# Layer 2 keys in written order with statistics a batch ahead; layer 0 preparation with a third TensorE tap and sums of offset excess

## The chip, the core and the metric

The kernel runs on one core of one Trainium2 chip. The metric is device time in microseconds (us) of one execution, taken as the median over the runs. All data is float32.

The core's engines are TensorE (PE for the matmuls, PEld for its weight loads), VectorE (DVE), ScalarE (ACT), GpSimd (POOL) and SyncE (SP), which issues nearly all of the transfers. Each engine works through its own queue in order and waits on semaphores.

## What is computed

The input is eight images of 56 x 56 pixels with 128 channels. Four layers follow one another. Two parts of them matter here.

Layer 0 is a deformable convolution with a small MLP behind it. Its first part, which the kernel calls the preparation, computes for each image a projection and, from a depthwise 3 x 3 convolution, the offsets and masks of the sampling:

```python
xp = x @ w_in + b_in                                   # what is sampled
h  = conv_3x3_depthwise(x, dw_w) + dw_b                # nine taps per channel
h  = gelu(batch_norm(h))
offset = (h @ w_off + b_off)                           # 4 groups x 9 points x 2
mask   = softmax((h @ w_msk + b_msk), axis=-1)         # over the 9 points
y = sample_bilinear(xp, grid + offset, mask)           # deformable sampling
```

Layer 1 is a whitening of the channels. Layer 2 starts with self-attention in which keys, queries and values are one and the same projection:

```python
n = (t - mean(t)) / sqrt(var(t) + 1e-5)                # per token, 3136 tokens an image
h = n @ W_k.T                                          # 8 heads of 16
scores = h @ h.T / sqrt(16)                            # per head
t = t + softmax(scores) @ h @ W_o.T
```

Feed-forward parts with experts and a linear attention (layer 3) follow; the change doesn't touch them.

## The kernel before

The kernel works through its stages one after another: preparation of layer 0, sampling and MLP of layer 0, whitening, keys of layer 2, attention of layer 2, experts, and layer 3 with its experts. Some stages have an order written out by hand (`tc.manual_schedule`, the attention is one); in the others a planner orders each engine's instructions by the program's order and by estimated times. Both stages that the change touches are left to the planner.

**Preparation of layer 0** (in `conv_layer`, lines 200 to 398). A loop goes over the images, with three of them in flight. `image` (L256) loads an image, transposes it on TensorE into 28 columns of tokens (L266), copies it on ScalarE into a padded plane `xp` (L271) and stores a reordered copy `xT` (L276, L279). Two images share one padded plane; there are two such planes. `first_taps` does the first `NTE` of the nine taps of the depthwise convolution as matmuls with diagonal matrices (L315, seven chunks of 128x448), and ScalarE copies the sums to `acc` (L322). `other_taps` does the other taps on VectorE, one instruction over 128x3136 each (L327). `projection` (L288, L295) runs once per pair of images, in two halves: TensorE multiplies, VectorE adds the bias, and the result goes to `strips` in DRAM. `hidden` is the GELU on ScalarE (L341). `offsets` multiplies on TensorE (L356), adds the bias on VectorE (L363) into `om`, takes the largest and the smallest offset of the image into `far` (L365, L366), does the softmax of the masks (`mask_softmax`, L430 to L435, with its Exp on ScalarE at L432), and stores `om`.

The rows and columns around `strips` are filled with zeros by transfers that ScalarE issues (L240, L245).

At the end the largest of all `far` decides whether every offset is within one pixel (L398). If it is, `sample_near` runs, otherwise a general and much slower form.

**Keys of layer 2** (`attention_keys`, L1039 to L1133). A loop goes over the eight images, here called batches. For each:

1. The tokens are loaded from `y` into `t` in two transfers of 56 partitions each, in pieces of 512 bytes, so that token 112 i + p stands at partition p, column i (L1062); and they are written to `tok` in the order of the tokens (L1063).
2. VectorE takes statistics of 28 columns (L1067, L1068) and adds the epsilon (L1140); POOL takes the power of -1/2 (L1141, in `rsqrt`).
3. VectorE normalizes column by column (L112), TensorE transposes (L121), ScalarE copies groups of four columns to `xT` (L122).
4. TensorE computes the keys in 14 chunks of 128x448 (L1083). VectorE and ScalarE take turns in scaling and copying them to `kT` (L1091, L1087). `kT` has one buffer and is stored in two transfers (L1094).
5. TensorE computes the values in 25 tiles (L1098). VectorE and ScalarE take turns in copying them to `va` (L1108, L1106), which is stored in two transfers (L1110).
6. POOL squares the values (L1117), VectorE sums them and takes the largest (L1119, L1120). These become a bound that decides which form of the attention runs.

All transfers are issued by SP. `query_bound` (L2080 to L2104), a short chain for layer 3 that begins with a load on SP (L2088), stands behind the keys in the program; the attention follows it.

Of the kernel before, what the change touches and what calls it, by code (L numbers as in the profile page):

```python
# [8 lines left out]
F32 = mybir.dt.float32  # L9
# [9 lines left out]
S = IH * IW  # L19
# [16 lines left out]
R4 = 4 * C  # L36

NPX = 6
NTE = 2


WB, WCOLS, WSTEP, WITER, WEPS = 64, NB * S * C // 64, 9, 5, 0.01
# [85 lines left out]
def conv_layer(tc, k, x, w, z):  # L128
# [3 lines left out]
    with ExitStack() as ctx:  # L132
# [63 lines left out]
        gam = row_bc(nc, cp, w["gamma2"], T, "gam2r")  # L196
        nc.vector.tensor_tensor(q.sft2, q.sft2, gam, ALU.mult)

        far = cp.tile([T, 2 * n_batch], F32, name="far")
        near = cp.tile([1, 1], I32, name="near")  # L200
        with ExitStack() as pre:
            ip = pre.enter_context(tc.tile_pool(name="l0i", bufs=1))
# [11 lines left out]
                "b_om",  # L214
            )
            b_om = b_om.unsqueeze(1).to_broadcast([T, GT, 3 * GP])

            dw = ip.tile([C, 9], F32, name="dw")
            nc.sync.dma_start(dw, w["dw_w"].rearrange("c a b d -> c (a b d)"))
# [13 lines left out]
            nc.vector.tensor_tensor(bn_t, bn_t, bn_s, ALU.mult)  # L233
            nc.vector.tensor_tensor(bn_t, bn_t, bn_b, ALU.add)

            zero = ip.tile([NX * n_batch, 2 * SW * C], F32, name="zero")
            nc.gpsimd.memset(zero, 0.0)
            rows = q.strips.rearrange("n k y s c -> (n k) y (s c)")
            for y in (0, VW - 2):
                nc.scalar.dma_start(  # L240
                    rows[:, y : y + 2].rearrange("k y s -> k (y s)"), zero
                )
            for n in range(n_batch):
                for at in (q.strips[n, 0, :, :2], q.strips[n, NX - 1, :, SW - 2 :]):
                    nc.scalar.dma_start(  # L245
# [104 lines left out]
            def offsets(n, hT):  # L350

                om = hp.tile([T, NT, 3 * GP], F32, name="om")
                for r in range(PH):
                    p = ps.tile([T, GT, 3 * GP], F32, tag="m", name="p_om")
                    for i in range(GT):
                        nc.tensor.matmul(  # L356
                            p[:, i, :],
                            hT[:, r, i].rearrange("p a b -> p (a b)"),
                            w_om,
                            start=True,  # L360
                            stop=True,
                        )
                    nc.vector.tensor_tensor(om[:, r * GT : (r + 1) * GT, :], p, b_om, ALU.add)  # L363
                off = om[:, :, : 2 * GP]
                nc.vector.tensor_reduce(far[:, 2 * n : 2 * n + 1], off, AX.XY, ALU.max)  # L365
                nc.vector.tensor_reduce(  # L366
                    far[:, 2 * n + 1 : 2 * n + 2], off, AX.XY, ALU.min, negate=True
                )
                mask_softmax(nc, hp, om)
                nc.sync.dma_start(q.om[n], om)  # L370


# [22 lines left out]
            nc.tensor.transpose(p, top, k.ident[:T, :T])  # L395
            one = ip.tile([1, 1], F32, name="far_one")
            nc.vector.tensor_reduce(one, p, AX.X, ALU.max)
            nc.vector.tensor_scalar(near, one, 1.0, None, ALU.is_le)  # L398

        taken = nc.values_load(near[0:1, 0:1], min_val=0, max_val=1)  # L400
        with tc.If(taken > 0) as both:
# [634 lines left out]
    return [(t, min(128, S - 128 * t)) for t in range(KT)]  # L1036


def attention_keys(tc, k, w, yv, tok, kT_out, va_out, low, small):  # L1039

    nc = tc.nc
    n_b = yv.shape[1]
    with ExitStack() as ctx:
        cp = ctx.enter_context(tc.tile_pool(name="akc", bufs=1))
        bp = ctx.enter_context(tc.tile_pool(name="akb", bufs=2))
        ps = ctx.enter_context(tc.tile_pool(name="akp", bufs=6, space=PSUM))
        vas = []  # L1050
        for i in range(2):
            va = cp.tile([128, 2, KT, 4, 32], F32, name=f"va{i}")
# [3 lines left out]
            vas.append(va)  # L1056
        tops = cp.tile([128, n_b], F32, name="tops")
        wk = w.wk.rearrange("p h d -> p (h d)")
        for n in range(n_b):
            t_sb = bp.tile([T, NT, C], F32, name="t")  # L1060
            for h in range(2):
                nc.sync.dma_start(t_sb[h * IW : (h + 1) * IW], yv[h, n])  # L1062
            nc.sync.dma_start(tok[n].rearrange("(t p) c -> p t c", p=T), t_sb)  # L1063
            mv = bp.tile([T, NT, 2], F32, name="mv")
            st = bp.tile([T, NT, 6], F32, name="st")
            for i in range(NT):
                nc.vector.bn_stats(st[:, i], t_sb[:, i])  # L1067
                nc.vector.bn_aggr(mv[:, i], st[:, i])  # L1068
            rs = rsqrt(nc, k, bp, mv, NT)
            xT = bp.tile([C, S], F32, name="xT")  # L1070
            for g in range(NG):
                xn = bp.tile([T, GT, C], F32, name="xn")
                for i in range(GT):
                    normalize(nc, xn[:, i], t_sb[:, g * GT + i], mv, rs, g * GT + i)
                transpose_group(
                    nc, k, ps, "m", xT[:, g * QC : (g + 1) * QC], xn, nc.scalar.copy
                )
            kT = bp.tile([128, 2, S], F32, name="kT", bufs=1)
            for g in range(2):
                for c in range(NG):  # L1080
                    cols = slice(c * QC, (c + 1) * QC)
                    p = ps.tile([128, QC], F32, tag="m", name="p_h")
                    nc.tensor.matmul(  # L1083
                        p, wk[:, g * 128 : (g + 1) * 128], xT[:, cols], start=True, stop=True
                    )
                    if c % 2:
                        nc.scalar.activation(  # L1087
                            kT[:, g, cols], p, AF.Identity, bias=w.one16, scale=DK**-0.25
                        )
                    else:  # L1090
                        nc.vector.tensor_scalar(  # L1091
                            kT[:, g, cols], p, DK**-0.25, w.one16, ALU.mult, ALU.add
                        )
                nc.sync.dma_start(kT_out[n, g], kT[:, g])  # L1094
            va = vas[n % 2]
            for t, m in key_tiles():
                p = ps.tile([128, 2, 4, DK], F32, tag="m", name="p_v")
                nc.tensor.matmul(  # L1098
                    p[:m].rearrange("p g j d -> p (g j d)"),
                    xT[:, t * 128 : t * 128 + m],  # L1100
                    w.wv,
                    start=True,
                    stop=True,
                )
                if t % 2:
                    nc.scalar.copy(va[:m, :, t, :, :DK], p[:m])  # L1106
                else:
                    nc.vector.tensor_copy(va[:m, :, t, :, :DK], p[:m])  # L1108
            for g in range(2):
                nc.sync.dma_start(va_out[n, g], va[:, g].rearrange("p t j d -> p (t j d)"))  # L1110

            sq = bp.tile([128, 2 * KT * 4, DK], F32, name="sq", bufs=1)
            v = va.rearrange("p g t j d -> p (g t j) d")[:, :, :DK]
            nc.gpsimd.tensor_tensor(sq, v, v, ALU.mult)  # L1117
            top = bp.tile([128, 2 * KT * 4], F32, name="top")
            nc.vector.tensor_reduce(top, sq, AX.X, ALU.add)  # L1119
            nc.vector.tensor_reduce(tops[:, n : n + 1], top, AX.X, ALU.max)  # L1120

        col = cp.tile([128, 1], F32, name="top_c")
        nc.vector.tensor_reduce(col, tops, AX.X, ALU.max)
# [12 lines left out]
def rsqrt(nc, k, pool, mv, n):  # L1136

    m = mv.shape[0]
    rs = pool.tile([m, n], F32, name="rs")
    nc.vector.tensor_scalar(rs, mv[:, :, 1], EPS, None, ALU.add)  # L1140
    nc.gpsimd.tensor_tensor(rs, rs, k.mhalf[:m, :n], ALU.pow)  # L1141
    return rs
# [1081 lines left out]
def token_layers(tc, k, a, y, out):  # L2224
# [3 lines left out]
    with ExitStack() as ctx:  # L2228
# [13 lines left out]
        with tc.tile_pool(name="tlr", bufs=1) as rp:  # L2242
# [33 lines left out]
            yv = y.rearrange("(t a) n w c -> a n w t c", a=2)  # L2276
            low = cp.tile([128, 1], F32, name="low")
            small = cp.tile([1, 1], I32, name="small")
            attention_keys(tc, k, w, yv, tok, kT_d, va_d, low, small)
# [108 lines left out]
```

## Time and profile before

| | us |
|---|---|
| median of 3 runs | 7665.0 (7655.8 to 7673.1) |
| the profiled execution | 7657.9 |
| its span, first to last instruction | 7656.2 |
| layer 0 preparation, 0 to 433 of the span | 433 |
| layer 0 sampling and MLP, 433 to 1437 | 1004 |
| layer 1 whitening, 1437 to 1580 | 143 |
| layer 2 keys with their weights, 1580 to 1949 | 369 |
| layer 2 attention, 1949 to 6545 | 4596 |
| the rest | 1111 |

Over the span the mean granted clock of TensorE is 0.908 of full speed. TensorE is busy 84% of it, VectorE 69%, ScalarE 54%, POOL 38%; but these are means over stages with different limits, and a stage's own windows have to be read for what limits it.

A line of a group reads: line of the kernel, engine, operation, output and inputs with their shapes, number of instructions; then busy time in us and the mean duration of one in ns; then the idle time of the engine just before them, and whom it waited for. A matmul of float32 leaves two records in the trace. A line of the waits reads: who waited, for whom: us in total, how many times, the longest.

### The profile page before, as it was taken

The numbers are of one execution on the slowest core, as the hardware profiler recorded it, in microseconds if no ns is written. First come the engines' busy times: TensorE is split into PE (matmuls) and PEld (weight loads), VectorE is DVE, ScalarE is ACT, GpSimd is POOL, SyncE is SP. The second block draws the span as 40 slices with busy tenths as digits, with TensorE's granted clock in tenths as the row PEclk, the third lists the DMA queues.
The fourth block names the chain that finished last, engine by engine and source line by source line (L and its number), as shares of the span: only waits on it lengthen the run. The fifth ranks groups of instructions, "written<-read, shape, count | busy, mean of one in ns | idle before, by whom it ended". The sixth has DMA issues, their size and how long they took to land. (4 is left out here: it accounts for less than half of the span.)

```text
span 7656.2 us, 158331 instructions
## 1 busy us (share of the span) xinstructions
PE 6459.4 (84%) x59947; PEld 2867.8 (37%) x59947; DVE 5281.9 (69%) x9840; ACT 4163.3 (54%) x6499; POOL 2939.2 (38%) x2555
## 2 busy tenths in 40 slices
PE   6659999565899999999999999999999999556764
PEld 4446666333233333333333323323323323235542
DVE  7975564356677777777777777777777777356761
ACT  4424444122566666666666666666666666146750
POOL 0001111022344444444444444444444444333763
PEclk9768899776999999999999999999999999789877
DMA  5453343376787877778777778878778777544544
GB/s 156 135 121 78 85 97 65 83 227 215 191 207 191 197 188 192 197 190 195 197 191 192 197 187 197 198 188 196 195 191 197 190 185 181 198 111 113 137 134 142
DMA packets 737846, 1287.45 MB, mean 168 GB/s; under 512 B 119235, under 2 KB 504645, under 8 KB 730053
## 3 DMA queue, kind: packets, MB, share of 16 engines
q1 hardware_dynamic: 727092, 1260.77, 65.5%
q0 software_dynamic: 6144, 12.60, 0.5%
q8 instruction: 486, 7.96, 0.4%
q10 hardware_dynamic: 3824, 3.68, 0.2%
q14 instruction: 300, 2.45, 0.1%
HBM read 286.04 MB, written 197.81 MB: 63 GB/s over the span
## 5 line engine op out<-in xcount | busy, mean ns | idle before, releaser
L1260 ACT ACTIVATE e<-p_s 128x768 f32<-128x768 f32 (+2 forms) x3712 | 2887.8, 830 | 1588.2 <-PE p_s L1252 1320.1
L1298 POOL COPY x<-sq 32x1152 f32<-32x1152 f32 x1792 | 2062.2, 1151 | 2017.6 <-PE p_s L1252 1241.2
L1271 DVE STREAM_TRANSPOSE sq<-e 128x768 f32<-128x768 f32 x2688 | 2434.3, 950 | 516.0 <-ACT e L1260 258.9
L1252 PE MATMUL p_s<-q,kT 32*128 32x384 f32 (+2 forms) x14848 | 1892.8, 548 | 37.8 <-ACT e L1260 21.9
L1305 PE MATMUL av<-e,va 128*32 128x384 f32 (+2 forms) x14848 | 1646.5, 515 | 13.3 <-DVE acc L1328 8.3
L1305 PE MATMUL avx<-x,va 128*32 128x384 f32 x10752 | 1134.3, 494 | 62.2 <-issue 38.9
L1252 PEld LDWEIGHTS p_s<-q,kT 32*128 32x128 f32 (+1 forms) x14848 | 649.3, 181 | 1266.1 <-issue 837.7
L1305 PEld LDWEIGHTS av<-e,va 128*32 128x32 f32 (+1 forms) x14848 | 294.0, 108 | 1030.7 <-issue 936.9
L1305 PEld LDWEIGHTS avx<-x,va 128*32 128x32 f32 x10752 | 351.5, 111 | 642.4 <-issue 601.9
L609 POOL TENSOR_TENSOR rs<-rs,mhalf 112x4 f32<-112x4 f32 x112 | 116.1, 1036 | 789.8 <-DVE rs L608 789.8
L1324 DVE TENSOR_TENSOR acc<-acc,avx 128x384 f32<-128x384 f32 x336 | 183.8, 547 | 232.5 <-PE avx L1305 229.5
L121 PE MATMUL p_tr<-ident,xn 112*128 112x112 f32 x672 | 133.5, 338 | 188.6 <-DVE xn L112 141.8
L1141 POOL TENSOR_TENSOR rs<-rs,mhalf 112x4 f32<-112x4 f32 (+2 forms) x136 | 167.9, 1235 | 249.6 <-DVE ntop L1986 123.5
L525 ACT COPY wT<-p_w 88x448 f32<-88x448 f32 x152 | 137.8, 921 | 193.1 <-PE p_w L523 193.1
L2034 ACT ACTIVATE xn<-t,ms,rs 112x128 f32<-112x128 f32 x448 | 185.2, 487 | 76.2 <-DVE ms L2027 76.2
L327 DVE SCALAR_TENSOR_TENSOR acc<-xp,dw,acc 128x3136 f32<-128x3136 f32 x56 | 193.9, 3471 | 29.8 <-ACT acc L322 29.7
L637 PE MATMUL p_f<-x1T,w 128*128 128x448 f32 x448 | 209.4, 593 | 4.4 <-DVE x1T L632 2.8
L121 PEld LDWEIGHTS p_tr<-ident,xn 112*128 112x128 f32 x672 | 97.5, 167 | 282.0 <-issue 186.6
L523 PE MATMUL p_w<-ident,wide 112*88 112x112 f32 x896 | 146.6, 303 | 58.6 <-DMA px<-strips 34.1
L1394 POOL TENSOR_TENSOR rs_b<-rs_b,mhalf 128x3 f32<-128x3 f32 (+1 forms) x72 | 58.5, 815 | 356.5 <-DVE rs_b L1393 347.0
L621 DVE TENSOR_TENSOR y<-y,p_rs 128x448 f32<-128x448 f32 x112 | 69.3, 619 | 182.2 <-PE p_rs L614 182.2
L122 ACT COPY xT<-p_tr 128x448 f32<-128x448 f32 x112 | 59.6, 532 | 229.2 <-PE p_tr L121 204.5
(363 smaller groups left out, 7816.5 us busy)
## 6 DMA issues: line engine op xcount, KB each, us to landing
x<-sq SPq DMA_DIRECT2D x5376, 144.0 KB
w<-in_L_ffn_weight_dram SPq DMA_DIRECT2D x64, 1024.0 KB
px<-strips SPq DMA_DIRECT2D x64, 616.0 KB
va_d<-va SPq DMA_DIRECT2D x16, 1600.0 KB
xT_d<-xT SPq DMA_DIRECT2D x112, 224.0 KB
xT<-xT_d SPq DMA_DIRECT2D x112, 224.0 KB
kT_d<-kT SPq DMA_DIRECT2D x16, 1568.0 KB
t<-t_a SPq DMA_DIRECT2D x16, 1568.0 KB
```

Source lines behind the costliest of these rows:

```text
L121: nc.tensor.transpose(p[:, i, :], src[:, i, :], k.ident[:T, :T])
L327: nc.vector.scalar_tensor_tensor(acc, xp[:, j // 3 : j // 3 + IH, j % 3 : j % 3 + IW], dw[:, j : j + 1], acc, ALU.mult, ALU.add,)
L523: nc.tensor.transpose(p[:, g], around[:, :, g], k.ident[:T, :T])
L637: nc.tensor.matmul(p, q.w1[:, f * 128 : (f + 1) * 128], x1T, start=True, stop=True)
L1141: nc.gpsimd.tensor_tensor(rs, rs, k.mhalf[:m, :n], ALU.pow)
L1252: nc.tensor.matmul(ss[j // 2][:m, j % 2, :width], kT[rows, 128 * i : 128 * i + m], q[rows, :width], start=True, stop=True,)
L1260: nc.scalar.activation(e[:m, 2 * j : 2 * j + 2, :width], ss[j][:m, :, :width], AF.Exp)
L1271: nc.vector.transpose(sq[:, :, i, j : j + 2].rearrange("p s j c -> p j s c"), exps[u, b, a, i][:, j : j + 2, :QB].rearrange("p j (s c) -> ...
L1298: nc.gpsimd.tensor_copy(*moves.pop(0))
L1305: nc.tensor.matmul(out, keys[u, b][1][:m, i, j, :], e[j], start=start, stop=stop)
L1324: nc.vector.tensor_tensor(to, to, in_order(av), ALU.add)
L2034: nc.scalar.activation(out[:, i], x[:, i], AF.Identity, bias=ms[:, i : i + 1], scale=rs[:, i : i + 1])
```

## The change

In the preparation of layer 0:

- `NTE` goes from 2 to 3: the third tap moves from VectorE to TensorE.
- The two reductions of the offsets to their largest and smallest value are gone. In their place ScalarE runs four Relu activations per image, each over half of the offsets and with one sign, which sum up by how much the offsets exceed one. The condition for `sample_near` becomes that the largest sum is not above zero.
- The tile of zeros is half as large, and the four border rows of `strips` are filled by four transfers instead of two.

In the keys of layer 2:

- The whole stage is written in its own order on all engines (`manual_schedule`).
- The tokens are loaded so that row h of the image's left or right half stands in one partition: 56 partitions x 14 KB for each of the two halves. `tok` is written in the same form. The copy after the transposes puts the columns of `xT` into the order of the tokens, which makes it a copy with a stride.
- The load and the statistics of batch n + 1 are taken during batch n: the load is issued at its start, the statistics in groups of four between the matmuls of the keys.
- All 14 copies of the keys go to ScalarE, and `kT` has two buffers.
- The sums of the squares of batch n are taken on VectorE during batch n + 1, after its normalization.

The diff, cut to its core:

```diff
-NTE = 2
+NTE = 3
...
-        far = cp.tile([T, 2 * n_batch], F32, name="far")
+        far = cp.tile([T, 4 * n_batch], F32, name="far")
...
+            minus = ip.tile([T, 1], F32, name="minus")
+            nc.vector.memset(minus, -1.0)
...
-            zero = ip.tile([NX * n_batch, 2 * SW * C], F32, name="zero")
+            zero = ip.tile([NX * n_batch, SW * C], F32, name="zero")
...
-            for y in (0, VW - 2):
-                nc.scalar.dma_start(
-                    rows[:, y : y + 2].rearrange("k y s -> k (y s)"), zero
-                )
+            for y in (0, 1, VW - 2, VW - 1):
+                nc.scalar.dma_start(rows[:, y], zero)
...
-                nc.vector.tensor_reduce(far[:, 2 * n : 2 * n + 1], off, AX.XY, ALU.max)
-                nc.vector.tensor_reduce(
-                    far[:, 2 * n + 1 : 2 * n + 2], off, AX.XY, ALU.min, negate=True
-                )
                 mask_softmax(nc, hp, om)
+
+                over = ip.tile([T, NT // 2, 2 * GP], F32, name="over")
+                for a in range(4):
+                    nc.scalar.activation(
+                        over,
+                        off[:, a // 2 * NT // 2 : (a // 2 + 1) * NT // 2],
+                        AF.Relu,
+                        bias=minus,
+                        scale=1.0 - 2.0 * (a % 2),
+                        accum_out=far[:, 4 * n + a : 4 * n + a + 1],
+                    )
                 nc.sync.dma_start(q.om[n], om)
...
-            nc.vector.tensor_scalar(near, one, 1.0, None, ALU.is_le)
+            nc.vector.tensor_scalar(near, one, 0.0, None, ALU.is_le)
...
-def attention_keys(tc, k, w, yv, tok, kT_out, va_out, low, small):
+def attention_keys(tc, k, w, y, tok, kT_out, va_out, low, small):
...
+        ctx.enter_context(
+            tc.manual_schedule(
...
-        for n in range(n_b):
+        def statistics(n):
             t_sb = bp.tile([T, NT, C], F32, name="t")
-            for h in range(2):
-                nc.sync.dma_start(t_sb[h * IW : (h + 1) * IW], yv[h, n])
-            nc.sync.dma_start(tok[n].rearrange("(t p) c -> p t c", p=T), t_sb)
+            inner = tok[n].rearrange("(h f i) c -> f h i c", f=2, i=NT)
+            for f in range(2):
+                of = slice(f * IH, (f + 1) * IH)
+                nc.sync.dma_start(t_sb[of], y[:, n, f * NT : (f + 1) * NT])
+            yield
+            for f in range(2):
+                nc.sync.dma_start(inner[f], t_sb[f * IH : (f + 1) * IH])
             mv = bp.tile([T, NT, 2], F32, name="mv")
             st = bp.tile([T, NT, 6], F32, name="st")
             for i in range(NT):
                 nc.vector.bn_stats(st[:, i], t_sb[:, i])
                 nc.vector.bn_aggr(mv[:, i], st[:, i])
-            rs = rsqrt(nc, k, bp, mv, NT)
+                if i % GT == GT - 1:
+                    yield
+            stats[n] = t_sb, mv, rsqrt(nc, k, bp, mv, NT)
+
+        def largest(n):
+            sq = bp.tile([128, 2 * KT * 4, DK], F32, name="sq", bufs=1)
+            v = vas[n % 2].rearrange("p g t j d -> p (g t j) d")[:, :, :DK]
+            nc.gpsimd.tensor_tensor(sq, v, v, ALU.mult)
+            yield
+            top = bp.tile([128, 2 * KT * 4], F32, name="top")
+            nc.vector.tensor_reduce(top, sq, AX.X, ALU.add)
+            nc.vector.tensor_reduce(tops[:, n : n + 1], top, AX.X, ALU.max)
+
+        stats, tail = {}, []
+        ahead = [statistics(0)]
+        while ahead:
+            advance(ahead)
+        for n in range(n_b):
+            t_sb, mv, rs = stats.pop(n)
+            if n + 1 < n_b:
+                ahead.append(statistics(n + 1))
+                advance(ahead)
             xT = bp.tile([C, S], F32, name="xT")
+            by_place = xT.rearrange("c (h f i) -> c i f h", f=2, i=NT)
             for g in range(NG):
                 xn = bp.tile([T, GT, C], F32, name="xn")
                 for i in range(GT):
                     normalize(nc, xn[:, i], t_sb[:, g * GT + i], mv, rs, g * GT + i)
-                transpose_group(
-                    nc, k, ps, "m", xT[:, g * QC : (g + 1) * QC], xn, nc.scalar.copy
-                )
-            kT = bp.tile([128, 2, S], F32, name="kT", bufs=1)
+                p = ps.tile([C, GT, 2, IH], F32, tag="m", name="p_tr")
+                for i in range(GT):
+                    nc.tensor.transpose(
+                        p[:, i].rearrange("c f h -> c (f h)"), xn[:, i], k.ident[:T, :T]
+                    )
+                nc.scalar.copy(by_place[:, g * GT : (g + 1) * GT], p)
+            advance(tail)
+            kT = bp.tile([128, 2, S], F32, name="kT")
             for g in range(2):
                 for c in range(NG):
...
-                    if c % 2:
-                        nc.scalar.activation(
-                            kT[:, g, cols], p, AF.Identity, bias=w.one16, scale=DK**-0.25
-                        )
-                    else:
-                        nc.vector.tensor_scalar(
-                            kT[:, g, cols], p, DK**-0.25, w.one16, ALU.mult, ALU.add
-                        )
+                    advance(ahead)
+                    nc.scalar.activation(
+                        kT[:, g, cols], p, AF.Identity, bias=w.one16, scale=DK**-0.25
+                    )
                 nc.sync.dma_start(kT_out[n, g], kT[:, g])
...
-            sq = bp.tile([128, 2 * KT * 4, DK], F32, name="sq", bufs=1)
-            v = va.rearrange("p g t j d -> p (g t j) d")[:, :, :DK]
-            nc.gpsimd.tensor_tensor(sq, v, v, ALU.mult)
-            top = bp.tile([128, 2 * KT * 4], F32, name="top")
-            nc.vector.tensor_reduce(top, sq, AX.X, ALU.add)
-            nc.vector.tensor_reduce(tops[:, n : n + 1], top, AX.X, ALU.max)
+            tail.append(largest(n))
+            advance(tail)
+        while tail:
+            advance(tail)
```

`advance(gens)` resumes the first generator of a list up to its next `yield`, and drops it when it has ended.

More of the change, by code (lines that the diff above doesn't have):

```diff
@@ L1036, in key_tiles @@
     return [(t, min(128, S - 128 * t)) for t in range(KT)]
-def attention_keys(tc, k, w, yv, tok, kT_out, va_out, low, small):
+def attention_keys(tc, k, w, y, tok, kT_out, va_out, low, small):
     nc = tc.nc
-    n_b = yv.shape[1]
+    n_b = y.shape[1]
     with ExitStack() as ctx:
@@ L1049, in attention_keys @@
         ps = ctx.enter_context(tc.tile_pool(name="akp", bufs=6, space=PSUM))
+        ctx.enter_context(
+            tc.manual_schedule(
+                engines={
+                    e.engine for e in (nc.tensor, nc.scalar, nc.vector, nc.gpsimd, nc.sync)
+                }
+            )
+        )
         vas = []
@@ L1074, in attention_keys @@
                     normalize(nc, xn[:, i], t_sb[:, g * GT + i], mv, rs, g * GT + i)
-                transpose_group(
-                    nc, k, ps, "m", xT[:, g * QC : (g + 1) * QC], xn, nc.scalar.copy
-                )
-            kT = bp.tile([128, 2, S], F32, name="kT", bufs=1)
+                p = ps.tile([C, GT, 2, IH], F32, tag="m", name="p_tr")
+                for i in range(GT):
+                    nc.tensor.transpose(
+                        p[:, i].rearrange("c f h -> c (f h)"), xn[:, i], k.ident[:T, :T]
+                    )
+                nc.scalar.copy(by_place[:, g * GT : (g + 1) * GT], p)
+            advance(tail)
+            kT = bp.tile([128, 2, S], F32, name="kT")
             for g in range(2):
@@ L1085, in attention_keys @@
                     )
-                    if c % 2:
-                        nc.scalar.activation(
-                            kT[:, g, cols], p, AF.Identity, bias=w.one16, scale=DK**-0.25
-                        )
-                    else:
-                        nc.vector.tensor_scalar(
-                            kT[:, g, cols], p, DK**-0.25, w.one16, ALU.mult, ALU.add
-                        )
+                    advance(ahead)
+                    nc.scalar.activation(
+                        kT[:, g, cols], p, AF.Identity, bias=w.one16, scale=DK**-0.25
+                    )
                 nc.sync.dma_start(kT_out[n, g], kT[:, g])
+            assert not ahead
             va = vas[n % 2]
@@ L2278, in token_layers @@
             small = cp.tile([1, 1], I32, name="small")
-            attention_keys(tc, k, w, yv, tok, kT_d, va_d, low, small)
+            attention_keys(tc, k, w, y, tok, kT_d, va_d, low, small)
         pooled = [cp.tile([C, n_b, E], F32, name=f"pooled{i}") for i in range(2)]
```

## The prediction

> **What bounds the two stages now.** I first cut the span into stages, with the view of busy time by windows. Columns: window and length, busy us of PE, PEld, DVE, ACT and POOL, granted clock, DMA share, GB/s.
>
> ```profile
> 0.00:433.00 433.00, 261.88 (x1345) 206.09 (x1345) 372.65 (x257) 187.09 (x248) 13.68 (x9) 0.82 0.54 148
> ...
> 1580.00:1949.00 369.00, 203.71 (x866) 135.24 (x866) 238.96 (x891) 85.66 (x200) 91.03 (x23) 0.70 0.69 216
> ```
>
> The diff touches only these: layer 0 preparation (433 us) and layer 2 keys (369 us). The other 6854 us stay as they are. The two behave differently. In the first, VectorE fills nearly all of the time once started; in the second, no engine reaches 65%, so waits set its length.
>
> **Layer 0.** A window over one pair of images, and the VectorE groups from 60 to 420 us:
>
> ```profile
> 213.00:305.00 92.00, 66.54 (x337) 51.13 (x336) 89.00 (x57) 47.47 (x62) 0.00 (x0) 0.83 0.52 149
> ```
> ```profile
> L327 DVE SCALAR_TENSOR_TENSOR acc<-xp,dw,acc 128x3136 f32<-128x3136 f32 x55 | 190.4, 3471 | 1.2 <-ACT acc L322 1.1
> L295 DVE TENSOR_TENSOR pj<-p_in,b_inr 113x512 f32<-113x512 f32 x56 | 36.0, 687 | 14.4 <-PE p_in L288 14.4
> L363 DVE TENSOR_TENSOR om<-p_om,b_om 112x432 f32<-112x432 f32 x56 | 32.2, 606 | 4.8 <-PE p_om L356 4.5
> L365 DVE TENSOR_REDUCE far<-om 112x1 f32<-112x2016 f32 x8 | 18.0, 2247 | 0.0
> L366 DVE TENSOR_REDUCE far<-om 112x1 f32<-112x2016 f32 x8 | 17.9, 2238 | 0.0
> ```
>
> See 89 of 92 us on VectorE: a pair of images costs what its VectorE work costs. TensorE has 25 us of slack per pair, ScalarE 45.
>
> **Layer 2 keys.** The view of who waited for whom, over 1595 to 1975:
>
> ```profile
> POOL sq L1117 <- DVE va L1108: 205.6, 8, 26.4
> ...
> PE p_tr L121 <- DVE xn L112: 141.8, 8, 29.0
> ...
> DVE xn L112 <- POOL rs L1141: 32.4, 8, 5.0
> ...
> DVE top L1119 <- POOL sq L1117: 16.9, 5, 5.7
> ```
>
> TensorE stands still 141.8 us, eight times, until a batch is normalized. In the TensorE timeline the batches start at 1614.1, 1650.7, 1690.9, 1733.5, 1787.6, 1824.4, 1864.8 and 1907.5: 36.5 to 54.1 us, mean 41.9. A batch is a chain: normalize and the three groups of matmuls (24.8 us, 1690.4 to 1715.2), then squares on POOL (5.5), their sums (3.8), the rest of the next batch's statistics, the power on POOL (4.8), normalize. The longest gaps (54 us) are where the next t lands late:
>
> ```profile
> 1716.00:1724.00 8.00, 0.00 (x0) 0.00 (x0) 5.14 (x19) 0.00 (x0) 5.12 (x1) 0.75 1.02 410
> 1726.00:1736.00 10.00, 2.47 (x10) 1.83 (x10) 5.05 (x28) 0.81 (x2) 4.79 (x1) 0.50 0.91 195
> ```
>
> The first window moves rows of 12.5 KB of keys and values, 128 partitions wide, at 410 GB/s; the second moves t, 56 partitions by 512 bytes, at 195: same DMA share, half the bytes. Piece size need not be the reason. Whitening loads rows of 14 KB into 64 partitions, and is no faster:
>
> ```profile
> 1454.00:1458.00 4.00, 0.60 (x3) 0.41 (x3) 0.00 (x0) 0.00 (x0) 0.00 (x0) 0.50 0.99 215
> ```
>
> **What the Trainium skill says.** "SBUF — State Buffer", section "Who interferes with whom": a VectorE tensor_scalar in a two-port mode and a GpSimd instruction exclude each other for a whole instruction; whichever starts later waits; reductions don't contend. The trace agrees:
>
> ```profile
> 1639.70 5.52 POOL L1117 TENSOR_TENSOR sq<-va 128x3200 f32<-128x3200 f32 x1 [26.04 <-DVE va L1108]
> ```
> ```profile
> 1640.27 4.99 DVE L1140 TENSOR_SCALAR rs<-mv 112x28 f32<-112x28 f32 x1
> 1645.26 3.49 DVE L1119 TENSOR_REDUCE top<-sq 128x200 f32<-128x3200 f32 x1
> ```
>
> The tiny rs, 0.18 us elsewhere, takes 4.99, until the squares end; normalize is a tensor_scalar of the same kind. "ScalarE: Activation LUTs", section "Table sets: the hidden batching unit": relu is in every table set, so the new Relus load no table; a load takes 1283 ns here and no run shows a Relu yet. That page's section "What ACT_TABLE_LOAD costs" prices an activation with a bias column at 280 + 0.833 ns per element: 1.12 us for 1008, as an estimate; the trace's Exp of that size takes 1.04.
>
> **Layer 0, part by part.** Removed from VectorE: one of seven taps per image, 8 x 3.47 = 27.8 us, and both offset reductions, 8 x (2.25 + 2.24) = 35.9. Together 63.7, or 15.9 per pair: 92 to 76. Added to TensorE: 14 records of 128x448 per image. The timeline has 28 in 10.7 us, so +5.35 per image, 43 in all, and 66.5 + 10.7 = 77 per pair. **TensorE and VectorE then tie**, so not all 15.9 comes back. VectorE waits at present 3 us per pair for TensorE's projections and offsets; I take 5 more, period 81, gain 11 per pair. Bounds: 4 (each engine waits in turn) and 15.9. Three steady pairs stand between 121 and 397. In the last (305 to 397) TensorE is busy only 48.7, so it gains about 15: together 11 + 11 + 15 = 37. The first 121 us gain nothing: TensorE must finish three images (+16) before the projections that VectorE now waits for from 100 to 121, which cancels the shorter VectorE work. In the tail (403 to 425) four reductions go, 9 us; two images' Relus come, four each of 1.04 to 1.12 plus an accumulator read of 0.2 (L2162), 4.9 us per image; they need only the offsets and fit where ScalarE waits 15.3 and 14.1 us for L431. If they queue ahead of an Exp, or behind it, I lose up to 5: net +5, from 0 to 9. Relus elsewhere: 9.8 per pair on ScalarE, 47.5 to 57, below 76; cover is that slack, and without it they delay the GELUs by up to 4.9 per image. The zero rows become four DMAs on ScalarE's queue instead of two (0.92 each): +1.8, hidden before 21.9 where ScalarE waits for bn_v, else it delays the first image copy at 39.9; I take it as lost. The halved memset is off the path. Sum 37 + 5 - 2 = **40 us**, bounds 10 and 62.
>
> **Layer 2, part by part.** Reads of y and writes of tok become rows of 14 KB, still 56 partitions in each DMA. So I price t (1.57 MB) as whitening's loads, 7.3 us at 215 GB/s (3.8 at 410 the low end, 8 as now the high one); tok at the 303 of whitening's stores (1545 to 1582), 5.2; keys and values, 6.34 MB at 410, 15.5. A batch is 28 us of DMA. The first t, landed at 1601.1, gains 1.5 (0 to 6). The next batch's t is issued behind the last batch's va (8 us), so it lands 8 + 7.3 + 2, some 17.5 us after a batch begins. On SP, tok waits for that landing, with this batch's keys queued behind it; they are ready only at 19 us, so that costs nothing, but DMA idles some 2 us: 30 in all.
>
> In written order VectorE does, per batch: normalize 28 x 0.26 = 7.3, sums of the last squares 3.8, statistics 7.3 and rs 0.2, then 13 copies of va at the pace of the value matmuls, 5.9. The 14 key copies all go to ScalarE: 14 x 0.63 = 8.8 within 10.5 of key matmuls. Its seven copies into xT now write with a stride; the strided copies L525 take 0.92 against 0.53, still under the 1.04 of four normalizations: +0.4 after the last. The sum is 24.5, TensorE's own 24.8. But the squares start when va ends, which is when normalize wants to start: either normalize waits 5.5, or the squares run after it and the sums (next on VectorE) wait 5.5. Both give **30.3**. Statistics want t at 16.6 and get it at 17.5; the power (4.8) after them ends at 30, just hidden. VectorE and DMA tie, so I take **31 us**. Low end 25 (no conflict, t at 410), high end 36 (t at 24).
>
> First normalize 1613.7 - 1.5 = 1612.2; eight batches 25 + 7 x 31 = 242, so values end near 1854 instead of 1932.7: 79 gained. The final squares and sums stay (10.6). The query bound's load now stands behind all of va on SP, and its chain may end 0 to 6 us after the keys' own: -3. Sum **76 us**, bounds 40 and 120.
>
> **Total**: 7657.9 (the profiled run: span 7656.2 and 1.7 around it) - 40 - 76 = 7542. The median of the runs shown is 7 higher, so I name **7549**.
>
> **Rivals.** (1) The port conflict vanishes (POOL slips between VectorE's instructions), t moves at 410, and layer 0 stays VectorE-bound: 26 per batch, -113, and -55: 7497. For it: TensorE and VectorE need only 25; against: the 4.99 us above. (2) Layer 0 turns TensorE-bound at a granted clock of 0.9: 77 / 0.9 = 86 per pair, 18 in three, 15 with the ends; keys as forecast: 7574. For it: TensorE waits 73.6 us for VectorE's p_in evacuations today. (3) Keys wait for t, 36 per batch: -40, and layer 0 -35: 7590. For it: t stands behind va. (4) Slower: SP stops at its first unready transfer, and t, 56 long rows, spreads badly over the DMA engines. A batch is then t's landing + statistics 7.5 + power 4.8. At 40 GB/s t lands at 48: 60 per batch, 25 + 7 x 60 = 445 against 319, +124, less 40: 7750. It decides from a landing at 35, 63 GB/s; whitening's 215 speaks against it. That near sampling is no longer chosen I exclude: a sum of excess of zero is the old condition.
>
> **How the numbers follow.** A measurement here tells about 0.2%, 15 us. Forecast 0.55, rival 1 0.13, rival 2 0.17, rival 3 0.10, rival 4 0.03, between it and rival 3 with no measurable change 0.02. The range reaches over rivals 1 to 3, the ends of the unknown costs partly cancelling: 7490 to 7610. Faster 0.95, same 0.02, slower 0.03.
>
> **What would show it.** Layer 0: six taps per image and no far reductions on VectorE, 42 records of p_dw per image instead of 28, pairs 81 apart, stage end near 393. Keys: batches 31 apart, a 5 us normalize or a 5 us wait of the sums on squares, t near 215 GB/s and landing about when statistics want it. A period of 26, or above 36, would break the keys' step; pairs still 92 apart the first.

## The result and the profile after

The change makes the kernel 1.2% faster: 7567.0 us median (7556.6 to 7580.3) against 7660.4 (7644.5 to 7673.1) for the kernel before in the same series, a ratio of 0.988 with a 95% interval of 0.9854 to 0.9907. The forecast was 7549, with a range of 7490 to 7610: a gain of 116 us, of which 93 came. The profiled execution took 7573.9 us, with a span of 7572.2, 84.0 less than before.

Line numbers below are those of the kernel after, where nothing else is said. Two marks cut the span: the first instruction of the sampling (`hat`), and the time from the issue of the first load of `t` to the first load of the attention's keys, called "the keys" here.

| | before | after | gain | forecast |
|---|---|---|---|---|
| sampling begins at | 443.3 | 405.1 | 38.1 | 40 |
| sampling to first load of t | 1145.8 | 1144.7 | 1.1 | 0 |
| the keys | 359.6 | 312.1 | 47.5 | 76 |
| the rest | | | -2.8 | 0 |

Layer 0 came out as forecast; the keys gave 28.5 us less. The windows that answer to those of before (window and length, busy us of PE, PEld, DVE, ACT and POOL, granted clock, DMA share, GB/s):

```profile
0.00:395.00 395.00, 298.54 (x1457) 227.83 (x1457) 311.92 (x235) 222.09 (x312) 12.83 (x9) 0.90 0.61 165
205.10:284.50 79.40, 74.26 (x366) 55.97 (x366) 70.91 (x49) 51.67 (x74) 0.00 (x0) 0.96 0.57 157
1550.00:1862.00 312.00, 217.48 (x865) 141.11 (x864) 243.53 (x824) 151.43 (x264) 82.98 (x17) 0.76 0.72 250
```

The second is one pair of images in the preparation: 79.4 us where it took 92, and now TensorE, at 74.3, is busier than VectorE. Groups of the preparation between 60 and 385, and below them what VectorE waited for in the projections:

```profile
L327 DVE SCALAR_TENSOR_TENSOR acc<-xp,dw,acc 128x3136 f32<-128x3136 f32 x48 | 166.6, 3472 | 36.3 <-ACT acc L322 36.0
...
L369 ACT ACTIVATE over<-om,minus 112x1008 f32<-112x1008 f32 x32 | 36.0, 1126 | 30.5 <-DVE om L363 30.3
...
L369 ACT ACTIVATION_READ_ACCUMULATOR over<-om,minus 112x1 f32 x32 | 6.2, 192 | 0.0
```
```profile
DVE pj L295 <- PE p_in L288: 26.4, 31, 0.9
```

There are six taps per image left on VectorE, and the two reductions are gone. A Relu takes 1.13 us, as estimated (1.12), and its accumulator read 0.19. VectorE's wait for the projections rose from 14.4 us (before, 60 to 420) to 26.4.

In the keys, who waited for whom from 1540 to 1870 (us in total, times, longest):

```profile
PE p_tr L1124 <- DVE xn L112: 67.5, 10, 23.3
...
DVE st L1089 <- DMA t<-y: 18.5, 7, 6.3
...
DVE xn L112 <- POOL rs L1183: 7.4, 6, 5.0
```

TensorE's standstill fell from 141.8 to 67.5, VectorE's wait for the power from 32.4 to 7.4. The batches (their first normalize on VectorE) start at 1577.1, 1605.8, 1642.5, 1676.9, 1710.9, 1745.2, 1779.3 and 1813.5, and in the steady part 34.2 us apart, not the 31 of the forecast. One of these batches in the timeline (start, length, engine, line, operation):

```profile
1710.86 12.53 DVE L112 TENSOR_SCALAR xn<-t,mv,rs 112x128 f32<-112x128 f32 x28 [0.16 <-POOL rs L1183]
1710.87 5.52 POOL L1101 TENSOR_TENSOR sq<-va 128x3200 f32<-128x3200 f32 x1
...
1717.83 7.09 ACT L1127 COPY xT<-p_tr 128x448 f32<-128x448 f32 x7 [7.51 <-PE p_tr L1124]
...
1724.98 12.67 PE L1134 MATMUL p_h<-xT,wk 128*128 128x448 f32 x28 [1.08 <-ACT xT L1127]
...
1728.91 0.29 DVE L1089 BATCH_NORM_STATS2 st<-t 112x6 f32<-112x128 f32 x1 [1.73 <-DMA t<-y]
...
1740.35 4.80 POOL L1183 TENSOR_TENSOR rs<-rs,mhalf 112x28 f32<-112x28 f32 x1 [23.97 <-DVE rs L1182]
...
1744.43 0.28 DVE L1156 COPY va<-p_v 64x128 f32<-64x128 f32 x1 [0.29 <-PE p_v L1146]
...
1745.19 5.53 DVE L112 TENSOR_SCALAR xn<-t,mv,rs 112x128 f32<-112x128 f32 x1 [0.48 <-POOL rs L1183]
```

**Two chains run through this batch, and they end 0.4 us apart.** The first goes through VectorE and POOL: normalize 12.5 (7.2 and a stall of 5.3 beside the squares), sums 3.8, wait for t 1.7, statistics and rs 11.4, power 4.8, with the gaps between them 34.3. The second goes through TensorE and ScalarE: normalize and the last copy into `xT` 14.1, key matmuls to the first value matmul 12.5, value matmuls with the last copy of `va` 7.2; that is at 1744.7, and the next normalize stands behind this copy on VectorE. Which of their terms are worth anything was the question of the experiments.

The load of `t` moved as forecast, no faster in rows of 14 KB than whitening's loads. The same columns again, at its middle:

```profile
1720.00:1724.00 4.00, 3.90 (x16) 2.58 (x15) 4.00 (x15) 3.92 (x5) 0.00 (x0) 0.50 0.88 211
```

### The profile page after: what moved, and what is told of

It is laid out like the page before. It is cut to its first block, busy times and chain, and to the rows that moved or that the text cites. A ratio compares the mean times of both kernels' runs of the same rounds, so it can differ in the third digit from the quotient of the medians.

```text
span 7572.2 us, 158626 instructions
## 1 busy us (share of the span) xinstructions
PE 6518.1 (86%) x60059; PEld 2902.3 (38%) x60059; DVE 5228.3 (69%) x9754; ACT 4265.3 (56%) x6627; POOL 2942.0 (39%) x2555
## 5 line engine op out<-in xcount | busy, mean ns | idle before, releaser
L1347 PE MATMUL av<-e,va 128*32 128x384 f32 (+2 forms) x14848 | 1644.8, 515 | 14.4 <-DVE acc L1370 9.1
L327 DVE SCALAR_TENSOR_TENSOR acc<-xp,dw,acc 128x3136 f32<-128x3136 f32 x48 | 166.6, 3472 | 36.3 <-ACT acc L322 36.0
L649 PE MATMUL p_f<-hid,w 128*128 128x448 f32 x448 | 180.3, 545 | 0.4 <-issue 0.4
L645 ACT ACTIVATE hid<-p_f,b 128x448 f32<-128x448 f32 x224 | 137.1, 640 | 57.3 <-PE p_f L644 49.6
L530 PEld LDWEIGHTS p_w<-ident,wide 112*88 112x88 f32 x896 | 120.9, 173 | 110.9 <-issue 77.8
```

The lines of the kernel that those rows point to most:

```text
L327: nc.vector.scalar_tensor_tensor(acc, xp[:, j // 3 : j // 3 + IH, j % 3 : j % 3 + IW], dw[:, j : j + 1], acc, ALU.mult, ALU.add,)
L530: nc.tensor.transpose(p[:, g], around[:, :, g], k.ident[:T, :T])
L649: nc.tensor.matmul(p[:, :QC], q.w2[:, f], hid[:, f], start=(f == 0), stop=(f == 3))
L1347: nc.tensor.matmul(out, keys[u, b][1][:m, i, j, :], e[j], start=start, stop=stop)
```

## The experiments

In the same units the change itself has a sampling that begins at 405.1, keys of 312.1 and a period of 34.2. All twelve are compared with the kernel before, in three series of four. Totals are medians, ratios have their 95% intervals; totals of one kernel spread by 10 to 40 us, so the lengths of the two stages, each from one profiled execution, are compared as well. They spread too: the same code of layer 0 began the sampling at 401.2 to 405.1 in nine executions, and the same code of the keys took 312.1 and 315.9, so that differences below 4 us in these two columns tell nothing. "Period" is the median of the seven distances between the stores of `va`; it was 34.2 and 34.3 for the same code.

| kernel | total | ratio to before | sampling begins | the keys | period |
|---|---|---|---|---|---|
| layer 0 only | 7621.4 | 0.9946 (0.9926 to 0.9966) | 402.1 | 360.2 | |
| keys only | 7619.1 | 0.9945 (0.9929 to 0.9962) | 444.0 | 315.9 | 34.3 |
| tap only | 7638.5, one run | | 419.9 | | |
| sums only | 7636.1, one run | | 418.1 | | |
| statistics grouped | 7566.2 | 0.9876 (0.9859 to 0.9892) | 402.8 | 305.0 | 34.1 |
| squares on ScalarE | 7577.2 | 0.9885 (0.9867 to 0.9903) | 404.1 | 315.2 | 36.3 |
| t early | 7575.1 | 0.9889 (0.9872 to 0.9905) | 403.3 | 310.5 | 34.1 |
| all three | 7524.8 | 0.9827 (0.9811 to 0.9843) | 401.2 | 266.4 | 28.5 |
| squares and t | 7527.4 | 0.9825 (0.9805 to 0.9844) | 402.9 | 273.0 | 28.6 |
| statistics and squares | 7544.5 | 0.9840 (0.9813 to 0.9867) | 404.0 | 278.8 | 30.7 |
| statistics and t | 7576.9 | 0.9883 (0.9863 to 0.9903) | 403.4 | 307.0 | 34.2 |
| all three, stores first | 7515.5 | 0.9808 (0.9792 to 0.9825) | 396.3 | 267.6 | 28.7 |

### The halves of the change

**Layer 0 only.** The hunks of `conv_layer` and `NTE`; `attention_keys` as before.

> Only the layer 0 half of the change: third TensorE tap, sums of offset excess in place of the two reductions, single-row zero writes; the keys stay as before. Theory (the two halves stand a millisecond apart and add up): about 38 us off, 7622 us, and the layer 2 keys take the time that they took before. Rival (the earlier end of layer 0 is partly given back by the planner's order of later stages): 25 us or less.

The sampling began 41.2 us earlier than in the kernel before, and the keys took 360.2 us, as before. The total fell by 34.5.

**Keys only.** The other half.

> Only the layer 2 keys in written order with statistics a batch ahead; layer 0 as before. Theory: the span of the keys alone falls by 47 us as in the whole change and some 3 are given back in the attention behind it, so 44 to 47 us off, 7615 us; batches of 34.3 us. Rival (the two halves help each other): the two halves together give clearly less or more than 93 us.

The keys took 43.7 us less, with a period of 34.3. The total fell by 36.8, and in the profiled execution the sampling, which is the same code, took 12 us longer; a total can't tell 37 from the 44 to 47 expected here. The two ratios multiply to 0.9891, inside the interval of the whole change (0.9854 to 0.9907). The halves are independent, within what a total can tell.

### Layer 0: the tap and the sums

```diff
-NTE = 2
+NTE = 3
```

> Of layer 0 only the third TensorE tap: eight vector taps of 3.47 us go, both reductions stay. VectorE has 85 us per pair of images left and TensorE 77, so VectorE still sets the pair. Theory (three steady pairs gain, the first does not): the sampling starts 18 to 21 us earlier. Rival (every VectorE instruction that goes counts in full): 28 us.

> Of layer 0 only the sums of offset excess on ScalarE (and the single-row zero writes), with two TensorE taps as before. VectorE loses 36 us, 9 per pair, and TensorE stays at 66 per pair. Theory (three steady pairs gain 9 each and the tail 5 more): the sampling starts 27 to 33 us earlier, so that this and the tap alone together gain more than the 38 us of both at once, because with both TensorE's 77 us per pair are as long as VectorE's 76. Rival (the two edits add up): 10 to 20 us here.

The second has the new `offsets`, `near` and `zero` with `NTE = 2`. With the tap alone the pairs are 84.9, 85.4 and 85.2 us long: VectorE's 85. With the sums alone 84.2, 83.8 and 83.5: VectorE's 83. With both (layer 0 only) they are 83.2, 78.6 and 77.8, where VectorE alone would give the forecast 76. Gains in the start of the sampling: 23.4 for the tap, 25.1 for the sums, and 38 to 42 for both (nine executions), less than their sum of 48.5. VectorE stands idle 2.9 to 3.3 us of each pair with the tap alone, and 7.5, 8.5 and 4.0 in the change. This is the tie of the two engines, and it costs most in the first pair; in the last TensorE is busy only 53 us of 78. Both single gains missed their expectation by a little: the tap gave 2 more than 21, the sums 2 less than 27.

For the sums the reason stands at the end of the stage. VectorE's last instruction there came 33.7 us earlier than before, but the sampling only 25.1. What SP waited for before it could load the offsets for the sampling (first in the sums only, then in the change, both from 384):

```profile
SPq L487 <- DMA om_d<-om: 6.7, 2, 3.6
SPq L487 <- DMA strips<-pj: 4.0, 2, 2.4
```
```profile
SPq L487 <- DMA strips<-pj: 3.2, 2, 2.7
```

In the kernel before this view has no wait for `strips`. The stores of the last pair's strips, at some 210 GB/s, seem to end last now, and the last store of offsets goes beside them. So of the 44 us by which VectorE ends earlier in the change, 5.7 are given back. The last experiment tests this.

### Keys: three repairs, one at a time

**Statistics grouped.**

```diff
-            for i in range(NT):
-                nc.vector.bn_stats(st[:, i], t_sb[:, i])
-                nc.vector.bn_aggr(mv[:, i], st[:, i])
-                if i % GT == GT - 1:
-                    yield
+            for i0 in range(0, NT, GT):
+                for i in range(i0, i0 + GT):
+                    nc.vector.bn_stats(st[:, i], t_sb[:, i])
+                for i in range(i0, i0 + GT):
+                    nc.vector.bn_aggr(mv[:, i], st[:, i])
+                yield
```

> The whole change, with the written order of the statistics changed: in each group of four, four bn_stats and then four bn_aggr, instead of each aggregate right behind its own statistics. Theory (an aggregate right behind the instruction whose result it reads costs 0.13 us more per pair, 3.7 us per batch): the stretch of 28 pairs falls from 11.2 to 7.4 us. In the steady batches the copies of va then end last, at most 0.5 to 1 us earlier than now, because TensorE and ScalarE reach them no sooner; the first batch gains 3.7 whole. About 10 us off the change's 7567, so 7557. Rival (the stretch is long because of what runs beside it, and stays over 10 us): no gain. Other rival (VectorE is the bound): 29 us off.

Statistics (L1067, L1089) and aggregates (L1068, L1090) in the timeline, first of the kernel before, then of the change: in the order that the planner chose, another column's statistics stand between a column's statistics and its aggregate.

```profile
1674.94 0.47 DVE L1067 BATCH_NORM_STATS2 st<-t 112x6 f32<-112x128 f32 x2
1675.34 0.15 DVE L1068 BATCH_NORM_AGGREGATE mv<-st 112x2 f32<-112x6 f32 x1
1675.42 0.25 DVE L1067 BATCH_NORM_STATS2 st<-t 112x6 f32<-112x128 f32 x1
1675.59 0.16 DVE L1068 BATCH_NORM_AGGREGATE mv<-st 112x2 f32<-112x6 f32 x1
1675.67 0.25 DVE L1067 BATCH_NORM_STATS2 st<-t 112x6 f32<-112x128 f32 x1
```
```profile
1738.30 0.18 DVE L1090 BATCH_NORM_AGGREGATE mv<-st 112x2 f32<-112x6 f32 x1
1738.40 0.26 DVE L1089 BATCH_NORM_STATS2 st<-t 112x6 f32<-112x128 f32 x1
1738.70 0.18 DVE L1090 BATCH_NORM_AGGREGATE mv<-st 112x2 f32<-112x6 f32 x1
1738.80 0.26 DVE L1089 BATCH_NORM_STATS2 st<-t 112x6 f32<-112x128 f32 x1
```

A column comes every 0.25 to 0.26 us in the first and every 0.39 in the second. Two lines with the repair, and then a batch of it:

```profile
1718.62 0.87 DVE L1090 BATCH_NORM_STATS2 st<-t 112x6 f32<-112x128 f32 x4 [2.13 <-DMA t<-y]
1719.41 0.36 DVE L1092 BATCH_NORM_AGGREGATE mv<-st 112x2 f32<-112x6 f32 x4
```
```profile
1700.17 12.52 DVE L112 TENSOR_SCALAR xn<-t,mv,rs 112x128 f32<-112x128 f32 x28
...
1714.28 13.02 PE L1135 MATMUL p_h<-xT,wk 128*128 128x448 f32 x28 [1.08 <-ACT xT L1128]
...
1726.27 4.79 POOL L1184 TENSOR_TENSOR rs<-rs,mhalf 112x28 f32<-112x28 f32 x1 [20.32 <-DVE rs L1183]
...
1734.08 0.28 DVE L1157 COPY va<-p_v 64x128 f32<-64x128 f32 x1 [0.30 <-PE p_v L1147]
1734.29 5.85 DVE L112 TENSOR_SCALAR xn<-t,mv,rs 112x128 f32<-112x128 f32 x2
```

The 28 pairs fell from 11.2 to 7.4 us. The power is now ready at 1731.1, and normalize starts at 1734.3, right behind the last copy of `va`: the second chain alone holds the batch, still 34.1 us long. The first batch gained its 3.3, the keys 7.1; the total, 7566.2 where 7557 was expected, did not move measurably.

**Squares on ScalarE.**

```diff
-            nc.gpsimd.tensor_tensor(sq, v, v, ALU.mult)
+            nc.scalar.activation(sq, v, AF.Square)
```

> The whole change, with the squares of va on ScalarE in place of GpSimd, so that the normalization no longer shares time with them. Theory: the normalization falls from 12.5 to 7.3 us, and VectorE then stands at its statistics until t lands, some 7 us in place of 1.7; the period stays near 34.3 us, the total within 4 us of the change's 7567. Rival (the sharing of 5.3 us per batch is on the path): 37 us off, 7530.

Normalize took 7.25 us, and nothing was gained: the keys took 315.2 us. The total, 7577.2, is 10 above the change's, within the spread. The waits from 1540 to 1870:

```profile
DVE st L1089 <- DMA t<-y: 46.4, 6, 8.3
...
PE p_v L1146 <- DVE va L1156: 28.7, 6, 6.0
```

VectorE now waits 7.7 us per batch for t, as the first theory had it. The statistics of a batch end about where they ended, 29.8 us after it begins (29.4 in the change). What the expectation didn't have is that the value matmuls, ready earlier, stand still behind VectorE, whose copies of `va` come after the statistics in its queue. After that they need some 6.5 us more, at first at a granted clock of 0.5, so the period grew to 36.3.

**t early.** Three buffers for `t`; in `statistics(n)` the load of image n + 1 is issued right behind the store of the tokens of image n.

```diff
...
+            if n == 0:
+                load(0)
...
             yield
+            t_sb = loaded.pop(n)
             for f in range(2):
                 nc.sync.dma_start(inner[f], t_sb[f * IH : (f + 1) * IH])
+            if n + 1 < n_b:
+                load(n + 1)
...
```

> The whole change, with t loaded a batch earlier still (three buffers; the load is issued right behind the store of the tokens of the batch before). Theory: VectorE's wait for t of 1.7 us goes, but the copies of va end last and come only 0.5 to 0.8 us earlier, so 4 to 6 us off, 7562. Rival (the wait is on the path in full): 12 us off, 7555. Other rival (the early load collides with the stores of kT and va): slower than the change.

The wait went from seven times to once, and the period stayed at 34.1. The keys' 310.5 us and the total of 7575.1, where 7562 was expected, show no gain. The period shows no collision either.

### Keys: the repairs together

**All three.**

> The whole change with all three: grouped statistics, squares on ScalarE, t a batch earlier. Theory (each of the three hides behind the others: VectorE's chain 23.6 us, ScalarE's and TensorE's 28, the transfers 28): period about 28.5 us, 44 us off the change's 7567, so 7523, far more than the sum of the three alone. Rival (transfers collide, or the squares on ScalarE hold its copies back): period 31 us or more, 25 us off or less.

```profile
1682.47 7.25 DVE L112 TENSOR_SCALAR xn<-t,mv,rs 112x128 f32<-112x128 f32 x28
...
1682.64 2.87 ACT L1110 ACTIVATE sq<-va 128x3200 f32<-128x3200 f32 x1 [0.47 <-DVE va L1165]
...
1691.46 12.44 PE L1143 MATMUL p_h<-xT,wk 128*128 128x448 f32 x28 [1.24 <-ACT xT L1136]
...
1710.89 1.35 DVE L112 TENSOR_SCALAR xn<-t,mv,rs 112x128 f32<-112x128 f32 x5
```

This batch takes 28.4 us; the forecast was about 28.5. Alone, the three shortened the keys by 7.1, -3.1 and 1.6 us; together by 45.7. The intervals of this kernel's ratio and of the change's don't overlap.

**Pairs of them.**

> The whole change with squares on ScalarE and t a batch earlier; the statistics stay as the change has them (aggregate right behind its statistics, 11.2 us). Theory (two chains of 34 us stand side by side: one through the normalization, TensorE and the copies of va, one through t, the statistics and the power): squares on ScalarE shorten the first to 28.4, the early t takes the second to 7.3 + 3.8 + 11.2 + 0.2 + 4.8 = 27.3, so the period is that of all three, 28.5; only the first batch keeps its 3.7 us. 7528. Rival (the pace of the statistics is on the path): 3.8 per batch more than all three, 7555.

> The whole change with grouped statistics and squares on ScalarE; t as the change loads it. Theory: the chain through t sets the period: landing 18.3 us after the batch begins, statistics 7.5, rs 0.2, power 4.8: 30.8 us. Against the 28.5 of all three that is 2.3 per batch: 7540. Rival (t costs nothing): 7525. Other rival (t is the bound in all of these kernels): 34 us per batch, 7563.

> The whole change with grouped statistics and t a batch earlier; squares stay on GpSimd. The chain through t and the statistics is then 12.5 + 3.8 + 7.4 + 0.2 + 4.8 = 28.7 us long. Theory (the other chain holds: normalization with its stall 12.5, the last transposes and copies 1.5, key matmuls 12.8, value matmuls with the last copy of va 7.2): the period stays 34.1, 7563, the first batch alone gaining. Rival (VectorE's own chain was the bound): 28.7, 7530.

Squares and t: period 28.6, forecast 28.5; total 7527.4, forecast 7528. The slow pace of the statistics then costs only the first batches: the keys take 6.6 us more than with all three, 3.7 were expected. Statistics and squares: period 30.7, forecast 30.8; VectorE waits for t seven times, 7.2 us each. Statistics and t: 34.2, forecast 34.1, though the chain through t is only 28.7 us long then; its total, 7576.9, missed the 7563 by 14, inside the spread of totals, while the keys' 307.0 agree with the 305.0 of the grouped statistics alone. All three periods are the longer of the two chains, as worked out ahead of the runs.

**All three, stores first.** In layer 0, for the last pair, the projection comes ahead of the last image's taps on VectorE.

```diff
+                    if n == n_batch - 1:
+                        for b in range(2):
+                            projection(n - 1, pairs[n // 2 % 2], b)
                     other_taps(place(n), accs[n])
-                    if n % 2 == 1:
+                    if n % 2 == 1 and n < n_batch - 1:
```

> All three, and in layer 0 the projection of the last pair of images ahead of the last image's taps on VectorE, so that the stores of its strips start some 20 us sooner. In the change the last instruction on VectorE comes 44 us earlier than before and the sampling only 38. Theory (the stores of the strips, at some 215 GB/s, hold the end of layer 0): sampling starts about 5 us earlier than with all three alone, 7520. Rival (the end is held by the softmax and the store of the last offsets alone, or the GELU of the last image loses its cover): no gain, or up to 5 us lost.

The sampling began at 396.3 instead of 401.2, 4.9 earlier; VectorE's work ended where it did (386.4 against 386.7), and SP no longer waited for `strips`. From VectorE's last instruction to the sampling it took 9.9 us, as in the kernel before (10.1), where it took 14.5 with all three. So the stores did hold the end of layer 0. This version is faster than the kernel before and than the change: 7515.5 us, 0.9808 of before. From all three alone its total can't be told apart.

## Why the prediction was right, and where it was not

The forecast of the total was right, though its keys were not. By the profiled executions the kernel is 32 us slower than forecast (7573.9 for 7542), and nearly all of that is in the keys. That the medians show only 18 of it comes from the spread of executions: the median of the change lies 7 us below its profiled execution, where 7 above was assumed. This part is luck.

**Layer 0, forecast 40, came 38.** The work taken from VectorE was as counted. The tie of TensorE and VectorE came: the forecast had 8 us of waiting per pair on VectorE, and the first two pairs had 7.5 and 8.5. The three pairs, forecast at 81, 81 and 77, took 84.7, 79.4 and 77.9, a gain of 34 for 37. The first 121 us gained 0.7, forecast nothing. In the tail VectorE's 9 us came, and the wait for the stores of the strips, which the forecast didn't have, took 5.7 back; that its net +5 came near is luck, for its loss was meant for the Relus. The Relus take 5.3 us per image; the forecast's 4.9 was added up too low, for its own terms give 5.0 to 5.3. No table load came with them: between 60 and 405 there are seven for the GELU and seven for the Exp, as before. With the four zero rows the first image copy came 0.8 later, forecast 2.

**Keys, forecast 76, came 47.5.** What held: t lands 18.0 us after a batch begins (forecast 17.5) and its rate is 211 GB/s (215); normalize loses 5.3 us beside the squares (5.5), and loses them no more when the squares leave POOL, as the Trainium skill, "SBUF — State Buffer", section "Who interferes with whom", has it of a tensor_scalar and a GpSimd instruction that overlap; the stores of `tok` hold up nothing in SP's queue. The load of the query bound was issued ahead of the last `va`, so its loss of 3 didn't come.

What failed are two terms of one sum, the period:

- *"statistics 7.3"*: 11.2. They had been taken from the trace of before at 0.26 us per column, where the planner puts the statistics of the next column between a column's statistics and its aggregate. The written order puts each aggregate right behind the result that it reads, and a column takes 0.39. With the group of four it is 0.26 again, which shows the cause. This lengthened the first chain from 30 to 34.3, and delayed the first normalize by 3.7.
- *"TensorE's own 24.8"*, which with the stall gave 30.3: 34. In the old order of the tokens a chunk of keys needed one group of four columns, and the key matmuls began before the last group was copied: 9.3 us from the last copy into `xT` to the end of the keys. In the new order every chunk of 448 needs all seven groups. The matmuls wait for the last copy, eight times, start at a granted clock of 0.5, and take 12.6. The step saw only the stride of the copies (+0.4). The value matmuls, to the last copy of `va`, take 7.2 instead of 6.2 (5.9 in the sum). That the order of the tokens costs these 3.3 us is read off the code and the two traces; no run undid it alone.

The lines of the second term, before and then after, each with windows that show the granted clock (the number before the DMA share). Before, the last copy into `xT` runs beside the key matmuls; after, all of them start behind it (1724.98 above).

```profile
1699.30 10.09 PE L1083 MATMUL p_h<-xT,wk 128*128 128x448 f32 x26
1699.55 0.53 ACT L122 COPY xT<-p_tr 128x448 f32<-128x448 f32 x1 [1.87 <-PE p_tr L121]
```
```profile
1700.00:1704.00 4.00, 4.00 (x12) 1.96 (x12) 1.37 (x2) 1.93 (x4) 0.00 (x0) 1.00 0.00 0
```
```profile
1729.42 8.90 ACT L1138 ACTIVATE kT<-p_h,one 128x448 f32<-128x448 f32 x12 [0.41 <-PE p_h L1134]
```
```profile
1726.00:1728.00 2.00, 2.00 (x4) 0.90 (x3) 1.15 (x2) 0.63 (x1) 0.00 (x0) 0.50 0.77 179
1728.00:1730.00 2.00, 2.00 (x6) 0.94 (x5) 1.01 (x5) 1.22 (x2) 0.00 (x0) 0.80 0.92 344
1730.00:1734.00 4.00, 4.00 (x12) 2.06 (x11) 3.62 (x21) 3.29 (x7) 0.00 (x0) 1.00 0.69 228
```

At the clock of 1.00 the chunks come every 0.74 us (12 copies in 8.9), so 14 of them would take 10.4. By this estimate 2.2 of the 3.3 us are the low clock, and the other 1.1 are the chunks that ran ahead of the last copy. TensorE was at 0.5 during the transposes in both kernels; in the kernel before it had reached 1.00 when the last copy ended, at 1700. Why it rose earlier there was not tried.

Each term makes its own chain 34 us long, which is why shortening one chain brought nothing in the steady batches. Together they make seven batches 3.4 us longer on average (34.4 for 31) and the first 3.4, and the first normalize comes about 4 late; less the 3 of the query bound that is the 28.5 missing.

**The rivals.** Nearest in time was rival 2 (7574), but not for its reason: it had layer 0 bound by TensorE at 86 per pair and the keys as forecast, and the pairs took 80.7 on average while the keys fell short. Rival 3 (7590) had the keys at 36 per batch waiting for t; with the squares on ScalarE this was nearly the mechanism, but in the change itself the wait is 1.7 us per batch and taking it away gains nothing. Rival 1, no port conflict, is refuted by the 5.3 us, and rival 4, a slow spread of t, by the 211 GB/s.

## What to carry to other kernels

Work out every chain that a batch closes over, through each engine and through the transfers, with the stalls in each: a period is the longest of them, and where two tie, repairs tried one at a time can look worthless. A new layout of data also changes which part of it the next step needs first; look for the overlap that this takes away. When a planner's order is written out by hand, look at what it had put between an instruction and the one that reads its result.

## What the runs showed of the hardware

- With a bn_aggr of 112x6 right behind its own bn_stats a pair takes 0.393 us, in groups of four 0.262. The Trainium skill, "VectorE: DVE Perf Modes", section "The DRAIN you can't avoid", says that a semaphore after each of eight copies cost nothing over one after the last. That is no measure of this case: here each second instruction is small and reads the result of the first, and the pair loses 0.13 us.
- The squares of 128x3200 take 5.52 us on POOL and 2.87 on ScalarE.
- Rows of 14 KB in 56 partitions moved at about 211 GB/s, little more than pieces of 512 bytes did (195); in the same kernel, from 1712 to 1716, the stores of `va`, rows of 12.5 KB in 128 partitions, moved at 432. The Trainium skill, "SBUF — State Buffer", section "Door 1: The DMA port swizzle (why `[64,N]` ≈ `[32,N]`)", says that partitions 0 to 63 reach 8 of 16 ports and puts the limit at some 218 and 436 GB/s. The two rates agree, though only one half of `t` lies in those partitions (the other in 56 to 111), and a load is compared with a store; that the ports are the reason was not tried here.
